# Moving TensorE's side pieces from the last two rounds of a block to the second round of the next

## The chip, the cores and the metric

The kernel runs on one core of a Trainium2 chip. The metric is the device time of one execution in microseconds, taken as the median of several executions. A core has five engines that run side by side, each working through its own queue of instructions in order: TensorE (PE in the profile; PEld is its weight load), VectorE (DVE), ScalarE (ACT), GpSimd (POOL) and SyncE (SP), which here issues most DMA transfers.

## The reference, cut to what matters

Two graph layers follow each other on 3327 nodes with 128 features, over one adjacency matrix.

```
# layer 0: graph attention
H = X @ W.T + b;  s = H @ a_s;  r = H @ a_r
e = leaky_relu(A * s + A * r.T, 0.2)
att = softmax(where(A > 0, e, -9e15), axis=1)
x = layernorm(x + att @ H)

# layer 1: attention with the adjacency as a bias, added twice
q = (x @ Wq.T).reshape(d, n, h)      # d = 128 "groups", n = 3327, h = 8
k, v likewise
a = einsum('dnh,dmh->dnm', q, k) * d**-0.5
a = softmax(a + adj + adj, axis=2)
out = einsum('dnm,dmh->dnh', a, v).reshape(n, h*d)
x = layernorm(x + out @ Wo.T)
```

The reshape in layer 1 is the heart of the matter: there are 128 attention matrices of 3327 x 3327, each with a head size of only 8. A group d needs the rows of q, k and v of only some 26 nodes, so group d can start when layer 0 has delivered those rows.

## The kernel before, in words

**Blocks.** Layer 1 takes four attention matrices at a time (`HG` = 4), so there are 32 groups. Each group has 7 blocks of 476 query columns (`NBLK`, `WB`), so there are 224 blocks. A block goes over 26 tiles of 128 keys (`NT`).

**Rounds.** A block is written out as 26 rounds (`rounds`, L707). Tiles come in stretches of three: i, i+1, i+2. The first tile of a stretch (`i in times`) has its exponentials taken by ScalarE straight out of PSUM (L994) and is then multiplied by a mask factor on GpSimd (L995). The other two get the mask added by VectorE out of PSUM (L997), and ScalarE takes the exponential later, in place (`exp_late`, L830). Round A of a stretch holds one half of tile i and one half of tile i+1, round B the other halves, round C both halves of tile i+2. So the first 24 rounds are eight stretches A, B, C; the last two, 24 and 25, are an A and a B alone, for tiles 24 and 25. Round 0 of the next block is again an A, round 1 a B, round 2 a C.

**TensorE in a round.** It computes four score matmuls (`scores`, L135), then at most one side piece (`work_tensor`, L912), then the products of a tile of four rounds earlier with v (`products`, L800, with `LAG` = 4). Scores of tiles i use one PSUM buffer of two banks (`pe`), those of the other tiles two such buffers (`pd`). The accumulator `av` and the side work have one bank each (`bank`, bufs=1).

**Side work.** Beside layer 1, the same loop carries the rest of the program in small pieces. `layer0(t)` delivers the rows t of layer 0: 26 products (L311), a VectorE chain with the layer norm, one transposition (L349) and 24 projections (L365), each of which VectorE must take out of `bank` before the next. `result(t)` finishes the rows t of the output: it loads `o` from DRAM (L450), makes nine transpositions (L460), divides on VectorE, makes eight projections (L479) and a layer norm (L486 to L495), and stores the rows (L500). `judge()` is one test of the inputs' ranges (L535 to L578), whose flag decides at the end whether a general fallback runs. All these stand in one queue, `main`, in order; a second queue, `aside`, prepares the masked weights of layer 0 on VectorE and GpSimd.

**Who decides when.** `lane(kind, n)` says how many pieces round n may take: kind "p" for TensorE, kind "d" for VectorE. A TensorE piece runs only if it is at the head of `main` at that round; if the head is a VectorE piece, the slot stays empty. `finish_to` (L933) runs everything that is due at once: 28 rounds before a group ends, for the rows that the next group reads, and once more after the last block, for all that is left. There each piece waits for the one before, since they share `bank` and are not spread over rounds.

```
units = [("x", load), ("w", 14), ("p", lambda: turn(7, 9, 0)), ...
units += [("p", lambda h=h: project(h)) for h in range(H)]
...
return units + [... ("d", scale)]        # scale: L495, then the store L500
```

In SyncE's queue, the store of one result (L500, which waits for L495) stands ahead of the load of the next result's `o` (L450).

Of the kernel before, what the change touches and what calls it, by code (L numbers as in the profile page):

```python
# [47 lines left out]
def kernel(  # L48
# [95 lines left out]
    def special():  # L144
        with ExitStack() as sx, tc.manual_schedule(engines=ALL):
# [571 lines left out]
            NR = len(rounds)  # L717
# [128 lines left out]
            def lane(kind, n):  # L846
                middle = n % 3 == 1 and 4 <= n < NR - 2
                if kind == "p":
                    return int(middle or n == 3 or n >= NR - 2)
                return int(middle or n == 0 or n >= NR - 2)  # L850

            made = [layer0(t) for t in range(1, NT)]
# [59 lines left out]
            def work_tensor(now, n):  # L912
                for _ in range(lane("p", n)):
                    if head("main", now) != "p":
                        break
                    run("main", now)

            def work(now, n):
                room, pool = lane("d", n), 1
                for row in ("main", "aside"):  # L920
                    while True:
                        kind = head(row, now)
                        if kind == "x":
                            pass
                        elif kind == "d" and room:
                            room -= 1
                        elif kind == "m" and pool:
                            pool -= 1
                        else:
                            break  # L930
                        run(row, now)
# [466 lines left out]
```

## Time and profile before

| | |
|---|---|
| time | 10420.47 us, median of 3 (10419.83 to 10420.89) |
| profiled span | 10418.4 us |
| mean granted TensorE clock | 0.996 |
| PE busy | 10195.1 us, 98% |
| ACT busy | 10088.8 us, 97% |
| DVE busy | 9410.9 us, 90% |
| POOL busy | 9223.5 us, 89% |

Read it with two cautions. Busy time is time in which an instruction is open on the engine, and matmuls overlap, so 98% is no measure of how much TensorE could be sped up. And with two engines at 97% or more, the share says nothing about which of them makes the other wait in a given round; that is read from the timeline, round by round. A round takes 10418.4 / 5824 = 1.79 us on average.

### The profile page before, as it was taken

Reading aid. Unit: us, or ns where it says so; the run is one execution under the profiler, and the core shown is the slowest. Engines: PE = TensorE matmul, PEld = TensorE weight load, DVE = VectorE, ACT = ScalarE, POOL = GpSimd, SP = SyncE. Lnnn points to the kernel's source line nnn. Section 1 sums busy time; section 2 is a strip of 40 time slices with the busy share of each in tenths; the row PEclk is TensorE's granted clock in tenths of the full one; section 3 lists DMA queues with packets and bytes.
Section 4 is the critical chain, followed back from the end, with each engine's and each line's share of the span. In section 5 each row is a group of like instructions: output and inputs, shape, how many; then the busy total and the mean of one; then the engine's idle time right before and its main releaser. Section 6 shows DMA issues by size and latency. Waiting matters only on the chain.

```text
span 10418.4 us, 195134 instructions
## 1 busy us (share of the span) xinstructions
PE 10195.1 (98%) x73245; PEld 3823.1 (37%) x73245; DVE 9410.9 (90%) x12247; ACT 10088.8 (97%) x8311; POOL 9223.5 (89%) x4395
## 2 busy tenths in 40 slices
PE   7999999999999999999999999999999999999998
PEld 3333333333333333333333333333333333333333
DVE  6999999999989999989999999999999899998887
ACT  6999999999999999999999999999999999999998
POOL 6988898889888899888898888888888888898887
PEclk8999999999999999999999999999999999999999
DMA  6655555555555555555555555555555555545554
GB/s 173 199 172 163 168 167 170 169 167 162 172 163 163 170 161 167 173 164 163 163 166 172 167 173 162 154 171 171 167 170 163 158 171 170 171 147 170 162 157 125
DMA packets 1176730, 1728.90 MB, mean 166 GB/s; under 512 B 121853, under 2 KB 1164382, under 8 KB 1171548
## 3 DMA queue, kind: packets, MB, share of 16 engines
q1 hardware_dynamic: 1174410, 1714.80, 55.5%
q8 instruction: 576, 9.44, 0.4%
q14 instruction: 383, 3.13, 0.1%
q10 hardware_dynamic: 1361, 1.53, 0.1%
HBM read 1611.92 MB, written 103.95 MB: 165 GB/s over the span
## 4 chain that ended last, share of the span: by engine, by line
PE 84%; ACT 8%; DVE 4%; issue 1%; DMA 1%; POOL 1%; SPq 0%; DVEq 0%; ACTq 0%; POOLq 0%
PE av L800 44%; PE scb L135 34%; ACT e L994 5%; ACT e L830 3%; PE bank L311 3%; DVE e L997 2%; PE bank L365 2%; POOL e L995 1%; PE bank L479 1%; DVE o L809 1%; DMA at<-in_adjT_dram 0%; PE bank L460 0%; DVE ot L469 0%; DMA k4b<-kT 0%; DVE lo L377 0%
## 5 line engine op out<-in xcount | busy, mean ns | idle before, releaser
L995 POOL TENSOR_TENSOR e<-e,at 128x952 f32<-128x952 f32 x4032 | 8966.3, 2234 | 1078.4 <-ACT e L994 903.2
L997 DVE TENSOR_TENSOR e<-scb,at 128x952 f32<-128x952 f32 (+1 forms) x7616 | 8417.6, 1144 | 857.5 <-PE scb L135 639.1
L830 ACT ACTIVATE e<-e 128x1904 f32<-128x1904 f32 (+2 forms) x4256 | 6875.3, 1621 | 17.5 <-DVE e L997 16.4
L800 PE MATMUL av<-e,v4b 128*32 128x476 f32 x46592 | 5905.4, 575 | 37.6 <-DVE o L809 30.7
L135 PE MATMUL scb<-q4b,k4b 32*128 32x476 f32 (+1 forms) x23296 | 4339.0, 592 | 124.5 <-ACT e L994 62.3
L135 PEld LDWEIGHTS scb<-q4b,k4b 32*128 32x128 f32 (+1 forms) x23296 | 2378.4, 296 | 4925.1 <-issue 1936.8
L994 ACT ACTIVATE e<-scb 128x952 f32<-128x952 f32 x4032 | 3871.4, 960 | 228.9 <-PE scb L135 133.7
L800 PEld LDWEIGHTS av<-e,v4b 128*32 128x32 f32 x46592 | 948.3, 108 | 1223.1 <-issue 770.1
L311 PE MATMUL bank<-hsb,w 128*128 128x129 f32 (+2 forms) x1300 | 318.4, 327 | 0.0
L311 PEld LDWEIGHTS bank<-hsb,w 128*128 128x128 f32 (+2 forms) x1300 | 193.7, 188 | 148.2 <-issue 147.8
L304 DVE TENSOR_SCALAR_CACHE_REDUCE dump<-a 128x384 bf16<-128x384 f32 (+2 forms) x468 | 247.3, 528 | 0.6
L284 DVE TENSOR_SCALAR_CACHE_REDUCE w<-trow,er 128x128 f32<-128x128 f32 (+1 forms) x650 | 220.9, 340 | 20.6 <-DMA trow<-td 12.6
L295 POOL TENSOR_TENSOR w<-w,a 128x384 f32<-128x384 f32 (+3 forms) x225 | 221.8, 986 | 0.1
L809 DVE COPY o<-av 128x476 f32<-128x476 f32 x224 | 145.9, 651 | 27.6 <-PE av L800 6.8
L377 DVE SCALAR_TENSOR_TENSOR lo<-bank,hi 128x128 fp32r<-128x128 f32 (+1 forms) x400 | 116.6, 291 | 13.8
L374 DVE TENSOR_SCALAR hi<-bank 128x128 fp32r<-128x128 f32 (+1 forms) x400 | 112.3, 281 | 0.0
L365 PE MATMUL bank<-wv,x1T 128*128 128x128 f32 (+1 forms) x400 | 98.5, 328 | 4.1 <-DVE vb L396 4.0
L479 PE MATMUL bank<-wo,ot 128*128 128x128 f32 (+1 forms) x416 | 101.5, 330 | 0.4 <-DVE ot L469 0.4
L365 PE MATMUL bank<-wk,x1T 128*128 128x128 f32 (+1 forms) x400 | 97.7, 326 | 3.7 <-DVE lo L377 2.5
L365 PE MATMUL bank<-wq,x1T 128*128 128x128 f32 (+1 forms) x400 | 97.7, 326 | 3.2 <-DVE lo L377 2.5
L479 PEld LDWEIGHTS bank<-wo,ot 128*128 128x128 f32 (+1 forms) x416 | 63.0, 193 | 46.1 <-issue 45.5
L365 PEld LDWEIGHTS bank<-wv,x1T 128*128 128x128 f32 (+1 forms) x400 | 60.0, 189 | 50.8 <-issue 40.4
(111 smaller groups left out, 820.1 us busy)
## 6 DMA issues: line engine op xcount, KB each, us to landing
at<-in_adjT_dram SPq DMA_DIRECT2D x1736, 476.0 KB
at<-ftd SPq DMA_DIRECT2D x1953, 238.0 KB
q4b<-qT SPq DMA_DIRECT2D x1788, 29.8 KB
k4b<-kT SPq DMA_DIRECT2D x126, 415.9 KB
at<-in_adjT_dram SPq DMA_DIRECT2D x217, 208.2 KB
at<-in_adjT_dram SPq DMA_DIRECT2D x56, 714.0 KB
a<-in_adjT_dram SPq DMA_DIRECT2D x50, 504.0 KB
ftd<-at SPq DMA_DIRECT2D x63, 238.0 KB
```

Source lines behind the costliest of these rows:

```text
L135: nc.tensor.matmul(dst, k4[32 * j : 32 * j + H4, i::NT], q4[32 * j : 32 * j + H4, :nb], start=True, stop=stop,)
L295: nc.gpsimd.tensor_tensor(w, w, s["a"][n][:, c0 - i0 : c1 - i0, :r], op=ALU.mult)
L304: nc.vector.tensor_scalar(z, a, float(k), None, op0=ALU.is_equal, op1=ALU.add, accum_out=even[:, t, at : at + 1])
L311: nc.tensor.matmul(s["p"][:r, : D + 1], s["w"][i // CW][: kr[i], i % CW, :r], hsb[: kr[i], i, :], start=(i == 0), stop=(i == NT - 1),)
L365: nc.tensor.matmul(s["b"][:r, :QW], s["xT"][:, :r], w[:, c : c + QW], start=True, stop=True)
L479: nc.tensor.matmul(s["b"][:r, :D], s["ot"][:, h, :r], wo[:, h, :], start=(h == 0), stop=(h == H - 1))
L800: nc.tensor.matmul(s.av[32 * j : 32 * j + 32, :], s.v4[:r, j, i * H1 : i * H1 + 32], e[:r, j, :], start=(s.left == NT - 1), stop=(s.left = ...
L809: nc.vector.tensor_copy(o4, s.av)
L830: nc.scalar.activation(e, e, AF.Exp, scale=2.0)
L994: nc.scalar.activation(eh, z[:r, :, :WB], AF.Exp, scale=2.0)
L995: nc.gpsimd.tensor_tensor(eh, eh, ah, op=ALU.mult)
L997: nc.vector.tensor_tensor(eh, z[:r, :, :WB], ah, op=ALU.add)
```

## The change

TensorE's side pieces may no longer run in the last two rounds of a block (24 and 25); instead one may run in round 1, the second round of the next block. The rule for VectorE's pieces (the line below) stays. It is meant to take TensorE work out of the seam between two blocks, where two stretches that begin with ScalarE's tiles follow each other closely, and to put it into a round B, as in the middle of the block.

```diff
             def lane(kind, n):
                 middle = n % 3 == 1 and 4 <= n < NR - 2
                 if kind == "p":
-                    return int(middle or n == 3 or n >= NR - 2)
+                    return int(middle or n == 1 or n == 3)
                 return int(middle or n == 0 or n >= NR - 2)
```

`NR` is 26. The slots for TensorE were rounds 3, 4, 7, 10, 13, 16, 19, 22, 24 and 25, ten in a block; they become rounds 1, 3, 4, 7, 10, 13, 16, 19 and 22, nine in a block.

## The prediction

> **What bounds the kernel now.** I read the page first, then the timelines of two seams (round 24 of a block to round 3 of the next), the timeline of the end, and the order of instructions on TensorE for both kernels. The page:
>
> ```profile
> PE 10195.1 (98%) x73245; PEld 3823.1 (37%) x73245; DVE 9410.9 (90%) x12247; ACT 10088.8 (97%) x8311; POOL 9223.5 (89%) x4395
> PE 84%; ACT 8%; DVE 4%; issue 1%; DMA 1%; POOL 1%; SPq 0%; DVEq 0%; ACTq 0%; POOLq 0%
> ```
>
> TensorE and ScalarE both look full and the chain runs mostly through PE. Which of them sets the pace depends on the round. Here is TensorE in a seam with side pieces in rounds 24 and 25 (columns: start us, length us, what, and in brackets idle time before it and its releaser):
>
> ```profile
> 5024.50 1.04 PE L135 MATMUL scb<-q4b,k4b 32*128 32x476 f32 x4
> 5025.47 0.49 PE L311 MATMUL bank<-hsb,w 128*128 128x129 f32 x2
> ...
> 5027.36 0.49 PE L311 MATMUL bank<-hsb,w 128*128 128x129 f32 x2
> ...
> 5030.46 0.60 PE L135 MATMUL scb<-q4b,k4b 32*128 32x476 f32 x4 [0.21 <-ACT e L994]
> ...
> 5034.01 0.61 PE L135 MATMUL scb<-q4b,k4b 32*128 32x476 f32 x4
> ```
>
> and ScalarE there, in round 25:
>
> ```profile
> 5027.46 0.96 ACT L994 ACTIVATE e<-scb 128x952 f32<-128x952 f32 x1 [0.41 <-PE scb L135]
> ```
>
> A piece delays TensorE by 0.42 us (5025.47 to the next start, 5025.89). The piece of round 24 makes ScalarE wait 0.41 us for the scores of round 25, and then, in round 1, TensorE waits for ScalarE: the single `pe` buffer is used in rounds 24, 25, 0 and 1 in succession. So the delay of the first piece is passed back and forth. This seam takes 5034.01 - 5024.50 = 9.51 us. A seam whose rounds 24 and 25 are empty, in the same phase of layer 0:
>
> ```profile
> 480.50 1.04 PE L135 MATMUL scb<-q4b,k4b 32*128 32x476 f32 x4
> ...
> 486.38 1.00 PE L800 MATMUL av<-e,v4b 128*32 128x476 f32 x8
> 487.31 1.01 PE L135 MATMUL scb<-q4b,k4b 32*128 32x476 f32 x4
> 488.25 1.21 PE L800 MATMUL av<-e,v4b 127*32 127x476 f32 x8
> 489.39 0.60 PE L135 MATMUL scb<-q4b,k4b 32*128 32x476 f32 x4
> ```
>
> It takes 489.39 - 480.50 = 8.89 us. The end of the program, after the last products:
>
> ```profile
> 10393.81 0.96 SPq L450 DMA_DIRECT2D o<-oT  x2
> ...
> 10398.70 1.08 PE L460 MATMUL bank<-identr,o 127*128 127x127 f32 x4 [7.92 <-DMA o<-oT]
> ...
> 10411.94 0.41 DVE L495 TENSOR_SCALAR x<-bank,st,root 127x128 f32<-127x128 f32 x1
> 10412.38 0.80 SPq L500 DMA_DIRECT2D out_dram<-x  x2
> ```
>
> Only one result is left over there. A result that nothing hides takes 4.9 us from the issue of its load to its first transposition, and 13.7 us (10398.70 to 10412.38) from there to its store.
>
> **What the Trainium skill says.** "Perfetto Trace Analysis", section Identifying the Most-Contended Engine: matmul busy share is no good measure of headroom. The trace agrees: the seam without pieces does the same attention work in 0.6 us less, though PE was "busy" before. The same page, section Matmuls: independent matmul groups should rotate through PSUM banks, so that emptying one overlaps the next group. Side work has one bank; the result at the end shows the consequence, every step waiting for the one before. The same page, section DMA Instruction — HWDGE (DVE, Sync): the sequencer waits for a DMA's semaphores before it issues, and the data movement lies outside the shown window. In the trace the issues of the `o` load last 0.96 us and TensorE waits to 4.9 us after their start.
>
> **The change, part by part.**
>
> *1. Seam: pieces leave rounds 24 and 25.* From the starts of the score matmuls (four to a round) I timed all 223 seams: 59 with products in both rounds, median 9.50 us; 65 with projections in both, 9.71 (there the second piece also waits for VectorE to empty `bank`); 43 with neither, 8.79. The sum is 2092.7 us, 9.38 each. Empty ones whose round 22 held a piece take mostly 8.88, the others 8.78. In the new order 176 blocks have a piece in round 22. So 176 x 8.88 + 47 x 8.78, plus 10 for those in which VectorE is full of small layer-norm steps (9.07 is the dearest common case), is 1985 us: **-108 us**.
>
> *2. Seam: a piece enters round 1.* I take it as nearly free. In the empty seam, the scores of round 2 last 1.01 instead of 0.60 us: their second pair waits for VectorE to empty a `pd` buffer, so TensorE has a hole of 0.41 us just after round 1, and the piece falls into it. The middle of the block shows this: rounds B and C last 1.47 + 1.88 us without a piece and 1.89 + 1.47 with one. And the products of round 2 wait for a late exponential anyway (1.21 instead of 1.01 us). What remains: the first scores of round 2 finish 0.4 us later, which delays VectorE and can hold up round 3 by some 0.1 us, where round 3 also has a piece (104 blocks): **+10 us**. The bounds are 0 and the full 0.42 us in 203 blocks, +85.
>
> *3. Middle of the block.* Rounds 3 to 22 hold 1268 pieces before and 1294 after. Rounds 3 to 23 take 35.49 us without pieces, 36.59 with six, 36.83 with eight. Grouping the new blocks by their number of pieces gives 10 us more than the same sum for the old ones. But 99 new blocks have their six in rounds 7 to 22, and the old blocks with just those take 36.49: 10 us less. **0 us**.
>
> *4. Forced work.* The queue moves on more slowly: in the projections, a slot follows another (3 after 1, 4 after 3) without VectorE having a turn between, so a block moves 7 projections instead of 9. Layer 0 is then late for groups 1 and 2: 11 and 4 projections are forced in one round, before it was 6 and 2. Before, those two rounds took 7.84 and 3.58 us instead of 1.47, which is 1.06 us for each piece: 7 more, **+7 us**. The judge leaves the loop, where it cost rounds of 4.06, 2.53, 2.35 and 2.28 us: **-4 us**.
>
> The loop in sum: -108 + 10 + 0 + 7 - 4 = **-95 us**.
>
> *5. What is left at the end.* For the same reason, the results fall behind. In the order of instructions, 225 transpositions L460 and 200 projections L479 stand before the last scores now, and 168 and 144 after the change. Behind the last products stand then the rest of one result (3 transpositions, 8 projections), seven whole results, and the judge. Nothing is left to hide them. In SyncE's queue, the load L450 of the next result stands behind the store L500, which waits for L495; behind the load wait the transpositions, and everything after them. So a result costs 13.7 (to the store) + 0.4 (its issue) + 4.4 to 4.9 (load; one transfer of 128 rows instead of two) = 18.7 us. First part: from the second transposition step of the old last result to its end, 10401.59 to 10412.35, less half a microsecond: 10.3 us. Seven results: 131. The judge: its steps run inside the loop now, and the view by source line has their durations (GpSimd squares 1.04, matmul about 0.66, reduction 0.67, ten to fifteen VectorE steps of 0.15 to 0.63): first total 0.8, three times 1.9, last reduction 0.8, tables and ranges 3.5, transposition and end 2: 12.8 us. Then flag and ending, 5 us. Together 159 us, against 27.6 now (10390.8 to 10418.4): **+132 us**.
>
> Sum: 10420.5 - 95 + 132 = **10458 us**, with the parts rounded.
>
> **Rivals.**
>
> *A. The loads of the leftover results are hidden,* since `o` is free after the last transposition, 8.3 us before the store. Then each costs 13.8, the end +97, the total 10420.5 - 95 + 97 = 10423, no change. The order of SyncE's queue speaks against it.
>
> *B. The piece in round 1 costs its full 0.42 us,* TensorE being the bound there. Then the seams save little: 10458 + 85 - 10 = 10533. The TensorE hole in round 2 speaks against it.
>
> *C. Faster:* besides A, the projection blocks with two pieces fewer run closer to ScalarE's pace (a block without pieces takes 44.3 us, one with nine projections 46.2) and save 50 us more than I counted: 10423 - 50 = 10373. For it speaks that 118 pieces leave the loop, which at 0.42 us would be 50 us; against it, that most of these pieces were taken out of the seam and are in part 1 already.
>
> **How the numbers follow.** Main forecast 0.74, A 0.13, B 0.08, C 0.05. Inside the main forecast the seams may be off by 0.1 us each (22 us) and a leftover result by 1 us (7 us): 10430 to 10486. To take in A and leave out B and C, the range is 10422 to 10492. Faster by 0.2% is below 10399.6, which is C: 0.04. Within 0.2% is up to 10441.3, A and the lower edge of the main one: 0.20. Slower: 0.76.
>
> **What would show it.** Right, if in the new profile the seams take about 8.9 us with a piece in round 1 and round 2 shorter by 0.4 us; if after the last products there are seven like stretches of 18 to 19 us, each with TensorE waiting for the DMA of `o`; and if PE's share falls in the last of the 40 slices. Wrong, if L460 waits for VectorE rather than the DMA there (A), or if seams stay above 9.2 us (B).

## The result, and the profile after

The changed kernel takes 10514.23 us (median of 6, 10511.06 to 10515.02) against 10420.43 for the kernel before (median of 6): a ratio of 1.0089, 95% interval 1.0076 to 1.0102. It is slower, as forecast, but by 94 us where 38 were forecast, and above the forecast's range of 10422 to 10492 us.

The page of the kernel after, its busy shares, and PE's busy tenths and granted clock over 40 slices:

```profile
PE 10194.1 (97%) x73245; PEld 3831.6 (36%) x73245; DVE 9392.4 (89%) x12247; ACT 10091.2 (96%) x8311; POOL 9222.5 (88%) x4395
...
PE   7999999999999999999999999999999999999995
...
PEclk8999999999999999999999999999999999999997
```

The busy times of PE, DVE, ACT and POOL are those of before to within 0.2%. The work is the same; only waits have been moved. In the last slice, PE's digit is 5 (8 before) and the clock's 7 (9 before): TensorE stands idle at the end. The view of waits, for TensorE (who waited for whom: us in total, times, longest):

```profile
PE av L800 <- DVE o L809: 62.6, 130, 0.6
PE bank L460 <- DMA o<-oT: 62.5, 7, 9.3
PE scb L135 <- ACT e L994: 28.7, 147, 0.9
```

Before, these were 30.7, 7.9 and 62.3 us. The wait for ScalarE in the seam has halved, as the change means it to. Two waits have grown instead: the one for the loads of the results left at the end, as forecast, and the one for VectorE's copy of the accumulator, which has doubled and was not forecast.

Four score matmuls start each round, so their start times give the length of every round. Summed over the blocks of the one profiled execution of each kernel (us; rounds 0 to 2 of the first block and round 24 of the last, 0.4 us in difference, are left out):

| stretch | before | after | difference | forecast |
|---|---|---|---|---|
| start of program to first scores | 87.9 | 85.9 | -2.0 | 0 |
| seams (rounds 24 to 2), 223 of them | 2092.7 | 1981.1 | -111.6 | -108 |
| of the next line: rounds 3 and 4, all blocks but the last | 818.8 | 866.3 | +47.5 | |
| rounds 3 to 23, 224 blocks | 8184.6 | 8260.3 | +75.7 | +13 |
| start of the last round to the end | 33.8 | 165.9 | +132.1 | +132 |

The terms for the seams and the end hold to within 4 us. The one for the middle of the block doesn't, and most of its loss sits in the first two rounds. The timeline of TensorE in a block of the projection phase, rounds 1 to 4, after:

```profile
4836.14 0.60 PE L135 MATMUL scb<-q4b,k4b 32*128 32x476 f32 x4
4836.67 0.49 PE L365 MATMUL bank<-wq,x1T 128*128 128x128 f32 x2
4837.09 1.01 PE L800 MATMUL av<-e,v4b 128*32 128x476 f32 x8
4838.02 0.60 PE L135 MATMUL scb<-q4b,k4b 32*128 32x476 f32 x4
4838.56 1.19 PE L800 MATMUL av<-e,v4b 127*32 127x476 f32 x8
4839.68 0.85 PE L135 MATMUL scb<-q4b,k4b 32*128 32x476 f32 x4
...
4841.40 0.61 PE L135 MATMUL scb<-q4b,k4b 32*128 32x476 f32 x4
4842.60 1.00 PE L800 MATMUL av<-e,v4b 128*32 128x476 f32 x8 [0.60 <-DVE o L809]
```

and VectorE there:

```profile
4838.73 3.26 DVE L997 TENSOR_TENSOR e<-scb,at 128x952 f32<-128x952 f32 x3 [0.76 <-ACT e L830]
4841.90 0.64 DVE L809 COPY o<-av 128x476 f32<-128x476 f32 x1
```

The piece (L365) does fall into round 1 as forecast, and the scores of round 2 then last 0.60 us instead of 1.01, with no hole. But they start and so finish later. VectorE begins the mask adds of round 2 0.71 us after those scores start and then has three adds to do without a break, two of round 2 and one of round 3. The bracket names ScalarE, whose exponential ended at the same moment, and so it is in 147 of 223 blocks. But the first add begins 0.70 to 0.71 us after the scores of round 2 in 221 of them, whichever engine is named, and in 218 in the kernel before, where no exponential L830 ends at that moment. So it is the scores that it waits for.

Two steps of TensorE wait for this row of adds. The second pair of scores in round 3 waits for the buffer of the first add (0.85 us instead of 0.60): over all blocks this pair begins 0.06 us after the end of that add and 0.24 us or more after the first pair (medians), where in the kernel with the piece in round 2, below, it follows the first pair at once. And the products of round 4 open a new accumulator, for which VectorE must first copy out the old one: L809 stands behind the third add. With no side piece in rounds 3 and 4 to fill the time, TensorE waits 0.60 us, and round 4 takes 2.14 us, while round 3 still takes 1.72. In a block with pieces in rounds 3 and 4 it is the other way round:

```profile
4702.64 0.83 PE L135 MATMUL scb<-q4b,k4b 32*128 32x476 f32 x4
4703.40 0.49 PE L311 MATMUL bank<-hsb,w 128*128 128x129 f32 x2
...
4704.76 0.60 PE L135 MATMUL scb<-q4b,k4b 32*128 32x476 f32 x4
```

Here round 3 takes 4704.76 - 4702.64 = 2.12 us, where a round 3 with a piece took 1.89 before, and round 4 keeps its 1.89.

The end, one leftover result in the timeline of after, all engines:

```profile
10362.13 0.41 SPq L450 DMA_DIRECT2D o<-oT  x1
...
10366.31 1.08 PE L460 MATMUL bank<-identr,o 128*128 128x128 f32 x4 [8.80 <-DMA o<-oT]
...
10379.24 0.41 DVE L495 TENSOR_SCALAR x<-bank,st,root 128x128 f32<-128x128 f32 x1
10379.68 0.34 SPq L500 DMA_DIRECT2D out_dram<-x  x1
10380.12 0.38 SPq L450 DMA_DIRECT2D o<-oT  x1
```

From load to load 10380.12 - 10362.13 = 18.0 us; the seven take 10490.42 - 10361.68 = 128.7 us from store to store, 18.4 each.

### The profile page after: what moved, and what is told of

Its sections match the earlier page's. It is cut to its first block, busy times and chain, and to the rows that moved or that the text cites. A ratio compares the mean times of both kernels' runs of the same rounds, so it can differ in the third digit from the quotient of the medians.

```text
span 10513.0 us, 195263 instructions
## 1 busy us (share of the span) xinstructions
PE 10194.1 (97%) x73245; PEld 3831.6 (36%) x73245; DVE 9392.4 (89%) x12247; ACT 10091.2 (96%) x8311; POOL 9222.5 (88%) x4395
## 4 chain that ended last, share of the span: by engine, by line
PE 80%; ACT 12%; DVE 4%; issue 2%; DMA 1%; POOL 1%; SPq 0%; DVEq 0%; ACTq 0%; POOLq 0%
PE av L800 41%; PE scb L135 32%; ACT e L830 6%; ACT e L994 6%; PE bank L311 2%; PE bank L365 2%; DVE e L997 2%; PE bank L479 1%; DVE o L809 1%; POOL e L995 1%; PE bank L460 0%; DMA at<-in_adjT_dram 0%; DMA o<-oT 0%; DVE ot L469 0%; DMA at<-ftd 0%
## 5 line engine op out<-in xcount | busy, mean ns | idle before, releaser
L830 ACT ACTIVATE e<-e 128x1904 f32<-128x1904 f32 (+2 forms) x4256 | 6873.9, 1621 | 17.4 <-DVE e L997 15.7
L800 PE MATMUL av<-e,v4b 128*32 128x476 f32 x46592 | 5901.3, 575 | 68.7 <-DVE o L809 62.6
L809 DVE COPY o<-av 128x476 f32<-128x476 f32 x224 | 145.2, 648 | 4.7 <-PE av L800 4.7
L460 PE MATMUL bank<-identr,o 128*128 128x128 f32 (+1 forms) x234 | 57.8, 337 | 82.9 <-DMA o<-oT 62.5
L365 PE MATMUL bank<-wv,x1T 128*128 128x128 f32 (+1 forms) x400 | 100.7, 335 | 5.4 <-DVE vb L396 4.7
L479 PE MATMUL bank<-wo,ot 128*128 128x128 f32 (+1 forms) x416 | 98.4, 351 | 3.1 <-DVE ot L469 3.1
L365 PE MATMUL bank<-wk,x1T 128*128 128x128 f32 (+1 forms) x400 | 97.9, 327 | 2.2 <-DVE lo L377 2.2
L365 PE MATMUL bank<-wq,x1T 128*128 128x128 f32 (+1 forms) x400 | 97.7, 326 | 0.0
```

The lines of the kernel that those rows point to most:

```text
L365: nc.tensor.matmul(s["b"][:r, :QW], s["xT"][:, :r], w[:, c : c + QW], start=True, stop=True)
L800: nc.tensor.matmul(s.av[32 * j : 32 * j + 32, :], s.v4[:r, j, i * H1 : i * H1 + 32], e[:r, j, :], start=(s.left == NT - 1), stop=(s.left = ...
L809: nc.vector.tensor_copy(o4, s.av)
L830: nc.scalar.activation(e, e, AF.Exp, scale=2.0)
```

## The experiments

Theory V: the piece of round 1 is paid by VectorE's row of adds, in rounds 3 and 4. Rival T: TensorE or ScalarE is short of time after the seam anyway, and gives back there what the seam saved. The runs differ from the changed kernel only in the lines shown. Times are medians of two to ten executions; lengths and sums of rounds are from the one that was profiled. "Round 3 with a piece" and "round 4 without" are medians over the blocks that have, or lack, a side piece in that round.

**No piece in the seam.**

```diff
-                    return int(middle or n == 1 or n == 3)
+                    return int(middle or n == 3)
```

> TensorE slots in rounds 3, 4, 7, 10, ..., 22 only: the changed kernel without the piece of round 1. Theory V (the piece of round 1 finishes the scores of round 2 0.4 us later; VectorE, which must then add three masks in a row before it copies the accumulator, is late, and TensorE waits for it in rounds 3 and 4): with the seam still near 8.85 us, round 3 with a piece falls back from 2.14 to 1.89 us, and round 4 without pieces in rounds 3 and 4 from 2.14 to about 1.75 us. Rival T (every round after the seam is short of TensorE or ScalarE time, and what the seam saves comes back in rounds 3 and 4 whatever runs in round 1): rounds 3 and 4 keep 2.14 us. Time under V: fewer slots leave eleven results and the judge behind the last products instead of eight and the judge, 3.3 x 18.3 = +60 us, more forced work +9 us, rounds 3 and 4 -65 us: about 10518. Under T: 10580.

Measured: 10559.64 us (before, in the same session: 10421.35; ratio 1.0133, 1.0104 to 1.0163). Round 3 with a piece is 1.89 us, round 4 without 1.78, at a seam of 8.88 in most blocks. So V, not T: with the same short seam, the waits are gone when round 1 is empty. The time missed V's 10518 by 42 us. I had left out that the pieces which no longer find a slot in round 1 run in rounds 3 to 22 (1447 pieces there instead of 1294), where they cost: the middle sums to 8236.4 us, 41 more than in the next run, of which 9 were forecast as forced work. The end is 66 us longer than in the changed kernel, near the forecast 60.

**The piece in round 2.**

```diff
-                    return int(middle or n == 1 or n == 3)
+                    return int(middle or n == 2 or n == 3)
```

> The piece of round 1 goes to round 2, behind its scores, all else as in the changed kernel: same slots in number, same results left at the end. Theory V: VectorE gets the scores of round 2 in time, so the waits of rounds 3 and 4 go (1.89 with a piece in round 3; about 1.75 in round 4 without); the piece shows in round 2 instead and makes the seam about 0.2 us longer (9.1 us). Blocks without pieces in rounds 3 and 4 gain 0.35 us, those with them nothing: about 99 x 0.35 = 35 us, total 10479. Theory T: the waits of rounds 3 and 4 stay and the seam grows by 0.2 us: 10514 + 45 = 10559.

Measured: 10497.63 us (ratio 1.0074, 1.0044 to 1.0103). The timeline of TensorE in the same phase, rounds 2 to 4:

```profile
4830.29 1.00 PE L135 MATMUL scb<-q4b,k4b 32*128 32x476 f32 x4
4831.22 0.49 PE L365 MATMUL bank<-wq,x1T 128*128 128x128 f32 x2
4831.64 1.01 PE L800 MATMUL av<-e,v4b 127*32 127x476 f32 x8
4832.58 0.61 PE L135 MATMUL scb<-q4b,k4b 32*128 32x476 f32 x4
...
4835.07 1.01 PE L800 MATMUL av<-e,v4b 128*32 128x476 f32 x8 [0.18 <-DVE o L809]
```

and VectorE there:

```profile
4830.99 3.47 DVE L997 TENSOR_TENSOR e<-scb,at 128x952 f32<-128x952 f32 x3 [0.35 <-PE scb L135]
4834.38 0.64 DVE L809 COPY o<-av 128x476 f32<-128x476 f32 x1
```

The adds again begin 0.70 us after the scores of round 2, but these are no longer late. Scores of round 3 are back at 0.61 us, and the wait for the copy is 0.18 instead of 0.60 (24.2 us over the program in the view of waits, 62.6 in the changed kernel). Over all blocks, rounds 3 and 4 sum to 801.6 us, 64.7 less than in the changed kernel; rounds 3 to 23 to 8195.4, 64.9 less. This kernel has the same number of pieces in every other round and the same end (165.3 us), so 65 us is the price of the late scores: 26 in round 3 of the 104 blocks with a piece there, 39 in the others, almost all of it in round 4. The seam is 9.10 us in blocks with a piece, and sums to 2027.1, 46 more. In the 99 blocks with a piece in the seam and none in rounds 3 and 4, the longer seam took back more than I had allowed: they gained 0.16 us each, not 0.35, hence 18 us more than V's number.

**The piece in round 0.**

```diff
-                    return int(middle or n == 1 or n == 3)
+                    return int(middle or n == 0 or n == 3)
```

> The piece of round 1 goes to round 0, where TensorE waits for ScalarE afterwards anyway (1.78 us for a round of 1.47). Theory V: scores of round 2 come 0.2 us later than without a piece, not 0.4; the seam stays at 8.9 us, round 3 with a piece is 1.9 us instead of 2.14, round 4 without pieces about 1.95 instead of 2.14, together -40 us. VectorE has a slot in round 0 too, so the queue moves faster: four results and the judge are left at the end instead of eight and the judge, 3.7 x 18.3 = -67 us; 62 more pieces in the loop +12 us: about 10420. Theory T: rounds 3 and 4 unchanged, 10460.

Measured: 10424.80 us, no different from the kernel before (ratio 1.0003, 0.9993 to 1.0013), 5 us off V's number. The seam is 9.01 us, round 3 with a piece 1.89, round 4 without 1.78. The end is 104.1 us long with four results left. The sum came out so close because two misses nearly cancel: the seams came out 26.5 us longer than in the changed kernel, where no change was forecast, and rounds 3 to 23 came out 57 us shorter, where 28 was forecast.

**Loads in front of the stores.** Only after the last products:

```diff
                     run(row, -1)
-                    tick(True)
+                    tick(mark is not None)
...
             finish_to(None, NG * total + LAG + 6)
+            tick(True)
```

> The changed kernel, but after the last products a result's store is put into SyncE's queue behind the loads of the next result. If the load of o is on the path of the leftover results because of its place behind the store, each of the seven full ones falls from 18.3 to about 13.9 us: -31 us, 10483. If the load is not what they wait for, no change: 10514.

Measured: 10482.61 us (ratio 1.0057, 1.0034 to 1.0080), at the first number. SyncE's queue in that trace:

```profile
10365.69 0.38 SPq L450 DMA_DIRECT2D o<-oT  x1
10370.19 0.32 SPq L454 DMA_DIRECT2D x1row<-x1d  x1
10373.99 0.34 SPq L500 DMA_DIRECT2D out_dram<-x  x1
10379.44 0.38 SPq L450 DMA_DIRECT2D o<-oT  x1
```

The load is issued 8.3 us before the store, and a result takes 10379.44 - 10365.69 = 13.75 us. The loop is unchanged (middle 8259.0 us). So the place in the queue was the cause of 4.6 us of each result.

**The copy ahead of the add.** The changed kernel, in round 3 alone:

```diff
                         work_tensor(g * total + at, n)
+                        if n == 3:
+                            waiting.append((s, order[n]))
+                            while len(waiting) > LAG:
+                                products(*waiting.pop(0))
                         for (i, h), z in zip(rnd, sc):
...
-                        waiting.append((s, order[n]))
+                        if n != 3:
+                            waiting.append((s, order[n]))
```

> The changed kernel with one thing turned round on VectorE: in round 3, the products are written out before the mask adds, so that the copy of the accumulator (L809) stands ahead of round 3's add on VectorE instead of behind it. TensorE's order is unchanged. Theory V says that in blocks without pieces in rounds 3 and 4, round 4 waits for this copy, behind three adds: round 4 falls from 2.14 to about 1.75 us there, while round 3 with a piece keeps its 2.14 us, since that wait is for a buffer of round 2's scores. The add now behind the copy is 1.2 us late and frees its buffer later, so round 5 grows, by up to 1.2 us; no gain in all. If round 4 keeps 2.14 us, the copy isn't what it waits for.

Measured: 10721.43 us (ratio 1.0288, 1.0269 to 1.0307). Round 4 without pieces falls from 2.14 to 1.90 us, round 3 with a piece keeps 2.14, round 5 grows from 1.58 or 1.48 to 2.52 us. VectorE's timeline (L1001 is the line of the adds here):

```profile
4932.60 2.21 DVE L1001 TENSOR_TENSOR e<-scb,at 128x952 f32<-128x952 f32 x2 [0.76 <-ACT e L830]
4935.41 0.65 DVE L809 COPY o<-av 128x476 f32<-128x476 f32 x1 [0.60 <-PE av L800]
4935.98 2.19 DVE L1001 TENSOR_TENSOR e<-scb,at 128x952 f32<-128x952 f32 x2
```

So the two waits have two causes, as V says: the copy for round 4, the buffer for round 3. Measured from the scores of round 2, the copy started only 0.37 us earlier, as it must wait for TensorE's last products (0.60 us idle), which fits that round 4 fell to 1.90 and not to 1.75. And the add put behind it holds up a score buffer for much longer: the loss is larger than the gain by 207 us in all.

**Slots in rounds 0 and 25, and in round 25 alone.**

```diff
-                    return int(middle or n == 1 or n == 3)
+                    return int(middle or n == 0 or n == 3 or n == NR - 1)
```

> TensorE slots in rounds 0, 3, 4, 7, 10, ..., 22 and 25: ten again. Side pieces stay out of round 24, where they delay the scores that ScalarE takes in round 25. Theory V: the seam becomes about 9.1 us (9.38 before, 8.9 after the change), rounds 3 and 4 stay at 1.89 and 1.78, and the queue moves as fast as in the kernel before, so one result is left at the end and the judge runs in the loop. Seams -70 us, the rest as before: about 10350. Rival: the piece of round 25 costs ScalarE the same wait as that of round 24, the seam stays at 9.3 us or more: 10400 or above.

```diff
-                    return int(middle or n == 1 or n == 3)
+                    return int(middle or n == 3 or n == NR - 1)
```

> TensorE slots in rounds 3, 4, 7, 10, ..., 22 and 25: of the kernel before, only the slot of round 24 is gone, and nothing is added in round 0 or 1. Tells the two removed pieces apart. If the piece of round 24 alone makes the seam long, the seam is 9.0 to 9.1 us (9.38 before); if both share it, 9.25 or more. Four results and the judge are left at the end (+70 us against the kernel before): 10420 with the first, 10460 with the second.

The first takes 10368.06 us (before, in that session: 10420.46; ratio 0.9949, 0.9935 to 0.9963): it beats both kernels. Seams sum to 2037.0 us, the middle to 8188.5, and the end to 33.5 us. It keeps half of what the change was for (seams -56 us of -112) and has neither of its two costs. It missed V's 10350 by 18 us, 14 of them in the seams. Its seams are 9.25 us in the projection phase, a little over the forecast 9.1, since the piece of round 0 must wait for VectorE to empty `bank` after that of round 25:

```profile
4820.79 0.49 PE L365 MATMUL bank<-wk,x1T 128*128 128x128 f32 x2 [0.20 <-DVE lo L377]
```

The second takes 10429.13 us (ratio 1.0008, 0.9998 to 1.0017), 9 us above the first number, with seams of 9.08 us in product and projection blocks, where 8.88 is the seam without pieces and 9.50 or 9.71 that with both. So the piece of round 25 costs 0.20 us, and that of round 24 the rest, 0.42 or more. The kernel before has seven seams with a product in round 24 alone, and they say the same: 9.30 us, 0.42 above 8.88. It is the piece of round 24 that is dear.

## Why the prediction was wrong

**Part 1, pieces leave the seam: right.** -111.6 us against -108; the common new seam is 8.88 us, as forecast. The reading behind it was thinner than it sounds: of the 19 empty seams of before whose round 22 held a piece, only 5 took 8.85 to 8.89 us and 11 took 8.97 to 9.08.

**Part 2, a piece enters round 1: right in what it named, wrong in its size, and this is the step that failed.** It said that the later scores of round 2 delay VectorE and can hold up round 3 "by some 0.1 us, where round 3 also has a piece (104 blocks)": +10 us. The runs show 65 us (changed kernel against the piece in round 2). Round 3 with a piece went from 1.89 to 2.14 us, so 0.25. And the blocks without pieces in rounds 3 and 4, which I had put at nothing, lost more, at round 4 (2.14 us, against 1.72 with the piece in round 2): 39 of the 65 us. I followed VectorE's delay to the score buffers but not to the next thing in its queue, the copy of the accumulator. That round is the only one of 26 in which TensorE needs it. The analogy to the middle of the block misled: a piece in a round B is nearly free there, but no copy follows two rounds later. This one term is 55 us too small, and the whole forecast was 56 us too low. The signs that the prediction had named for being right all came out (seams of 8.88 us, a round 2 of 1.66 instead of 2.08, seven stretches of 18.4, an idle last slice): none of them looked at rounds 3 and 4.

**Parts 3 and 4: right to within 8 us.** The rest of the middle is 75.7 - 64.9 = +10.8 us, against +3 in sum. Round 23, where the forced pieces stand, grew by 9.8 us (+7 forecast): its two forced rounds took 15.15 and 5.95 us, as many pieces as forecast but each a little dearer. One count was wrong: the slots in use fell by 100, from 1597 to 1497, not by 118: it seems that transpositions were counted singly, while most pieces of L460 make two.

**Part 5, what is left at the end: right.** +132.1 us against +132, though the errors of its parts cancel. The first, partly done result took 8.4 us (10.3), the seven 128.7 (131), judge and ending 22.6 (18): the judge's matmuls took 1.86 us a pair, where I had 0.66 us. So the agreement to the last microsecond is luck: each of the three is off by 2 to 5 us.

**The rivals.** A (hidden loads) fell: the seven waits for the DMA of `o` are in the view of waits, and hiding them took 31 us off. B, which gave the piece its full 0.42 us in TensorE's time, was wrong in its cause but nearer in its sum: it put 85 us on the piece, where the runs show 65. Its test, a seam above 9.2 us, looked at the wrong rounds. The range ended at 10492 and left it out; the time fell between the two. C (faster) fell as well: for it, the blocks with fewer projections had to save 50 us more than counted, and the rest of the middle grew by 10.8 us instead.

## What to carry to other kernels

A hole in one engine's timeline is free only until the work put into it delays what the others were waiting for: follow each delayed output through the whole queue of the engine that consumes it, to the next thing there that the first engine needs, including things that come once in many rounds. When slots for background work are moved, count how fast the background queue moves afterwards, since a slot that follows another without the other engine's turn between can stay empty; here 100 slots fewer were used in the loop, and the work left over cost 132 us at its end. And try the removal one by one: the piece of round 24 carried most of the seam's cost, so that moving it alone to a round where TensorE waits anyway won 52 us.

## What the runs showed of the hardware that I had not expected

TensorE's granted clock falls in the idle end of the program. The view of stretches, a window in the loop and one at the end, of the kernel after (columns: us, busy time and instructions of PE, PEld, DVE, ACT, POOL, then clock, DMA share, GB/s):

```profile
10240.00:10340.00 100.00, 98.61 (x714) 36.30 (x714) 88.88 (x99) 99.25 (x83) 88.61 (x41) 1.00 0.46 139
10360.00:10510.00 150.00, 52.13 (x184) 35.85 (x184) 50.98 (x193) 0.00 (x0) 4.16 (x4) 0.54 0.13 35
```

Sixteen projection matmuls L479 took 2.05 us right after the last products and 3.45 us one result later. The Trainium skill, "TensorE: Matmul & The Clock Gate", section What's actually happening, says that a clock gate passes a share of the pulses according to how busy the array has lately been; the trace agrees, with 0.54 over that window. The result that stood at the end of the kernel before had a clock of 0.50 over its 13.7 us already, so the price taken from it held for seven.
